# Counting a group once behind serial accumulating DMAs, and projecting in halves into the bank of the counts

## The chip, the core and the metric

The kernel runs on one core of one Trainium2 chip. The metric is the time of one execution on the device, in microseconds (us). Before the change the median of three runs is 3099.81 us (3097.14 to 3100.33). The core has five engines with a queue each, worked off in order: PE multiplies matrices into the output memory PSUM, which the kernel uses in banks of 512 float32 columns per partition; DVE and ACT work on its results and copy them out to SBUF; POOL adds tiles in SBUF and issues the accumulating DMAs; SP issues the other DMAs.

## The reference

Sixteen batches of 1024 rows and 256 columns go through two attention layers, each after a layer norm with ReLU, with a residual sum. Layer 0 has 4 heads, layer 1 has 8; the same 1024x1024 adjacency matrix of a batch masks both. Cut to what matters:

```python
h = max(layernorm(x), 0)
q, k, v = h @ Wq, h @ Wk, h @ Wv                  # per head
scores = where(adj > 0, q @ k.T / sqrt(D), -inf)
x = x + (softmax(scores) @ v) @ Wo + bo           # layer 0, then the same for layer 1
```

## The kernel before

All work is in float32, and the scores are kept transposed: keys lie on the partitions and 512 queries (one half `qh` of the rows) on the free axis. A **group** is one half of the queries and 128 of the 256 head columns (`g`): two heads of 64 columns in layer 0, four heads of 32 in layer 1. A layer of a batch thus has four groups, g0 to g3 in the order (qh 0, g 0), (0, 1), (1, 0), (1, 1). A group has 8 **steps** in layer 1 (4 in layer 0); a step makes four blocks of 128 keys by 512 queries.

What a step does: `scores` (L493 to L505) writes two pairs of banks from the pool `ps_s`, which has three pairs. `exponentials` masks each pair on DVE (L524) into a tile p, which frees the pair, and takes the exponential on ACT (L530). Two steps later (`LEAD`), `weigh` (L535) multiplies p by the values into the bank `po`. Even steps put their p into a tile of the pool tag `p0` with 7 buffers, odd ones into two half tiles of the tags `p10` and `p11` with 2 buffers each.

The softmax denominators are the sums of p over the keys. In layer 1 `count_steps` (L645) first has POOL add each odd step's p onto the even step's tile, in place (L659, two additions of 128x1024 each), after `weigh` has read both. That leaves four tiles per group, after the steps j = 1, 3, 5, 7. An accumulating DMA from POOL's queue (`accumulate`, L642) adds one such tile to another. `count` (L381) multiplies by a matrix of ones and so sums over the partitions; it writes the bank `pz`, which has a single buffer (the pool `ps_o` has one buffer per tag). `spread` (L404) copies that bank out on ACT (L407), sends the sums to another layout by DMA, and `invert` (L425), `fetch` and `normalize` (L447) take the reciprocal, bring it back and scale the group's output.

Before the change the groups g0, g1 and g2 of layer 1 are counted twice, once for j = 1 and 3 together and once for j = 5 and 7, and most of these counts are issued in two halves of 256 columns at successive steps (`halves`, L689). g3 is counted once. In layer 0 groups are added differently (`add_tiles`) and counted in pairs.

The inputs of a layer (norm, transpose, then `k`, `q` and `values` for each half of the rows) are made in steps of other batches. Norms are computed on ACT (L221) into one buffer `hn`, transposed in 32x32 blocks on DVE (L273), written to DRAM by a DMA as `turned` (L278) and read back as hT (L285). The projections `kq` (L289) and `values` (L341) each fill one pair of `ps_s`, with 4 matmul calls for k or q and 8 for values (a matmul call lies in the trace as two instructions), and ACT or DVE copies the pair out. `end_half` (L478) projects the finished half by Wo through a pair of `ps_s` too (py, L483).

The order of everything is written out by hand. Steps of all batches form one list: layer 0 of batch b+1 (16 steps), then layer 1 of batch b (32 steps), and so on. I call such a run of 32 layer-1 steps a **stage** and number its steps 0 to 31; step 32 is the first of the following layer 0. `later(i, f, ...)` files a function for step i, and `run` (L588) issues, for each step: the scores, the weighing of earlier steps, the due counts, the exponentials, the other due functions in the order in which they were filed, and last those named in `LARGE`. At an even step of layer 1 with a due function from `LARGE`, the weighing is put off to the next step. `gr.waits` and `at` give the distances from a group's last weighing to its counts and to spread, invert, fetch and normalize. The stage of batch b carries the layer-0 inputs of batch b+2, filed at c + ..., where c is the stage's step 0.

Of the kernel before, what the change touches and what calls it, by code (L numbers as in the profile page):

```python
# [21 lines left out]

LEAD = 2

LARGE = ("k", "q", "values", "end_half")
COUNTS = ("count", "count_added")


# [62 lines left out]
def fast_program(ctx, tc, a, w, loads, chk):  # L91
# [89 lines left out]
    class Inputs:  # L181
# [98 lines left out]
        def place_blocks(self, half):  # L280
# [3 lines left out]
            for k in range(4):  # L284
                nc.sync.dma_start(  # L285
                    hT[ts(k, 32)].rearrange("p c (g q) -> p c g q", q=P), blocks[k]
                )

        def kq(self, half, is_q):  # L289
            if half == 0 and not is_q:  # L290
                self.kT = actp.tile([P, 2, N], F32, tag="kT", name=f"kT_{self.n}")
                self.v = actp.tile([P, NT, E], F32, tag="v", name=f"v_{self.n}")
            if is_q:
                to = self.qT[half] = actp.tile(
                    [P, 2, 512], F32, tag="qT", bufs=3, name=f"qT_{self.n}_{half}"
                )
            else:
                to = self.kT[:, :, ts(half, 512)]
            wt = w.q if is_q else w.k
            pq = psum_pair(f"pq_{self.n}_{half}_{int(is_q)}")  # L300
            shared = self.layer == 0 and self.b == 0 and half == 0
            for m in range(2):
                for c in range(2):
                    nc.tensor.matmul(  # L304
                        pq[:, m, :], wt[self.layer][:, c, ts(m, P)], self.hT[half][:, c, :],
                        start=(c == 0), stop=(c == 1),
                    )
            if shared:
                nc.scalar.copy(to[:, 0, :], pq[:, 0, :])
                nc.vector.tensor_copy(to[:, 1, :], pq[:, 1, :])  # L310
            elif self.layer == 0:
                if is_q:
                    nc.vector.tensor_copy(to, pq)
                else:
                    nc.scalar.copy(to, pq)
            else:
                for m in range(2):
                    if is_q:
                        nc.vector.tensor_scalar_add(to[:, m, :], pq[:, m, :], w.bq[:, m : m + 1])
                    else:  # L320
                        nc.scalar.activation(
                            to[:, m, :], pq[:, m, :], AF.Identity, bias=w.bk[:, m : m + 1]
                        )

        def test(self):

            held = small.tile([P, 32], F32, tag="held", bufs=1, name=f"held_{self.n}")
            for i in range(self.sums.shape[1] // 32):
                for bound, op in ((SUM_MIN, ALU.is_ge), (SUM_MAX, ALU.is_le)):
# [2 lines left out]
                    )  # L332
                    nc.gpsimd.tensor_mul(chk, chk, held)

        def k(self, half):
            self.kq(half, False)

# [230 lines left out]
    class Stream:  # L568
# [76 lines left out]
        def count_steps(self, i, st):  # L645
# [7 lines left out]
            elif j % 2:  # L653
                one = self.steps[i - LEAD - 1].p
                if gr.last and not (gr.brief or gr.pairs) and j == 7:
                    self.accumulate(gr.two, gr.one)
                for k, of in enumerate(st.halves):
                    half = one[:, ts(k, 2), :]
                    nc.gpsimd.tensor_add(half, half, of)  # L659
                if gr.pairs and (st.last or gr.hurry):  # L660
                    self.later(i + 2, gr.count, one, j == 1, st.last)
                elif gr.pairs:
                    self.halves(i + 3, gr, one, j == 1, False)
                elif j == 1:
                    gr.one = one
                elif j == 3:
                    self.accumulate(one, gr.one)
                    gr.one = one
                    if not gr.last:
                        self.halves(i + gr.waits[0], gr, one, True, False)  # L670
                    if gr.brief:
                        self.later(i + 6, gr.count, one, True, False)
                elif gr.brief and j == 5:
                    self.halves(i + 5, gr, one, False, False)
                elif gr.brief:
                    self.later(i + 4, gr.count, one, False, st.last)
                elif j == 5:
                    gr.two = one
# [21 lines left out]
        def end_group(self, i, gr):  # L700
# [128 lines left out]
    def block_inputs(inp, half, turn, put, place, *at):  # L829

        later(turn, inp.turn_blocks, half)
        later(put, inp.put_blocks, half)
        later(place, inp.place_blocks, half)
        for i, f in zip(at, (inp.k, inp.q, inp.values)):
            later(i, f, half)


    for i, f, half in (0, inp.k, 1), (0, inp.values, 0), (0, inp.values, 1), (2, inp.q, 1):
# [16 lines left out]
    for b in range(B - 1):  # L855
# [5 lines left out]
            norms(mine, 1, a + 10, a + 11, a + 12, a + 13, whole=True)  # L861
            half_inputs(mine, 1, a + 15, c, c + 6, c + 2)
        else:
            norms(mine, 0, a - 20, a - 16, a - 15, a - 13, bias=a)
            block_inputs(mine, 0, a - 10, a - 8, a - 4, a, a + 2, a + 8)
            norms(mine, 1, a - 14, a - 10, a - 8, a - 6, bias=a + 6)
            block_inputs(mine, 1, a, a + 6, a + 7, c, c + (6 if b + 2 < B else 10), c + 2)
        for i, u in zip((0, 2, 4, 6, 7, 9, 11, 13), range(NT)):
            later(a + i, masks[b].second, u)
        if b + 2 < B:  # L870
# [2 lines left out]
            later(c, open_x, b + 2, 1)  # L873
            if b == 0:
                norms(other, 0, a + 12, a + 14, c, c + 1, bias=c + 34)
                block_inputs(other, 0, c + 2, c + 3, c + 4, c + 8, c + 16, c + 18)
                norms(other, 1, c + 3, c + 4, c + 6, c + 7, bias=c + 36)
                block_inputs(other, 1, c + 8, c + 9, c + 12, c + 22, c + 26, c + 30)
# [267 lines left out]
```

## Time and profile before

| | |
|---|---|
| median of the runs | 3099.81 us |
| profiled execution | 3096.61 us |
| its span, first to last instruction | 3094.8 us |
| granted TensorE clock | 0.999 of full |
| PE, DVE, ACT, POOL busy | 99%, 80%, 72%, 79% of the span |
| accumulating DMAs | 133, of 1 MB each |

The stages repeat: the same large item of a stage starts 189.4 us after that of the one before (438.37, 627.97 and 817.37 us for one py). Of these 189.4 us some 76 belong to the 16 steps of layer 0 and some 113 to the 32 steps of layer 1. In the timeline a row merges equal instructions that follow each other: start, time, engine, line, operation, tiles, shapes and number, and in brackets idle time before it with what ended it. The time of a step is read from the start of its scores to the start of the next step's scores. In the groups by shape, busy time counts overlapping instructions of one group once.

### The profile page before, as it was taken

Reading aid. Unit: us, or ns where it says so; the run is one execution under the profiler, and the core shown is the slowest. Engines: PE = TensorE matmul, PEld = TensorE weight load, DVE = VectorE, ACT = ScalarE, POOL = GpSimd, SP = SyncE. Lnnn points to the kernel's source line nnn. Section 1 sums busy time; section 2 is a strip of 40 time slices with the busy share of each in tenths; the row PEclk is TensorE's granted clock in tenths of the full one; section 3 lists DMA queues with packets and bytes.
Section 4 is the critical chain, followed back from the end, with each engine's and each line's share of the span. In section 5 each row is a group of like instructions: output and inputs, shape, how many; then the busy total and the mean of one; then the engine's idle time right before and its main releaser. Section 6 shows DMA issues by size and latency. Waiting matters only on the chain.

```text
span 3094.8 us, 47328 instructions
## 1 busy us (share of the span) xinstructions
PE 3074.0 (99%) x17406; PEld 1221.3 (39%) x17406; DVE 2474.6 (80%) x2698; ACT 2230.1 (72%) x2436; POOL 2436.5 (79%) x1554
## 2 busy tenths in 40 slices
PE   9999999999999999999999999999999999999998
PEld 4443433434334343343434334343343433434333
DVE  6778788887888878788787888878788787887777
ACT  5677777777777777778677677776777777776676
POOL 3578878787887878878788787887878778787787
PEclk9999999999999999999999999999999999999999
DMA  5215545454463544635445353554535545453331
GB/s 129 66 58 118 127 106 129 121 112 119 107 137 110 119 118 103 143 108 117 120 103 134 107 127 110 113 127 110 127 110 111 132 105 125 120 112 84 79 77 33
DMA packets 259230, 341.37 MB, mean 110 GB/s; under 512 B 58288, under 2 KB 218288, under 8 KB 241968
## 3 DMA queue, kind: packets, MB, share of 16 engines
q0 software_dynamic: 19152, 139.47, 22.6%
q1 hardware_dynamic: 238368, 197.51, 22.2%
q8 instruction: 138, 2.26, 0.3%
q10 hardware_dynamic: 1472, 1.31, 0.2%
q14 instruction: 100, 0.82, 0.1%
HBM read 149.95 MB, written 47.96 MB: 64 GB/s over the span
## 4 chain that ended last, share of the span: by engine, by line
PE 95%; DVE 2%; POOL 1%; DMA 1%; issue 1%; ACT 0%; SPq 0%; DVEq 0%; ACTq 0%; POOLq 0%
PE ps L501 31%; PE po L542 29%; PE pq L304 15%; PE pv L345 8%; PE py L483 7%; PE pz L387 4%; DVE p L524 1%; POOL p L659 1%; DMA inv<-vd 0%; DMA x<-in_x_dram 0%; SPq L420 0%; ACT p L530 0%; DMA sums<-s 0%; POOL cat L447 0%; DMA adj<-in_adj_dram 0%
## 5 line engine op out<-in xcount | busy, mean ns | idle before, releaser
L524 DVE SCALAR_TENSOR_TENSOR p<-mask,ps 128x1024 f32<-128x1024 fp8e5 x1536 | 1791.9, 1214 | 366.2 <-PE ps L501 348.5
L530 ACT ACTIVATE p<-p 128x1024 f32<-128x1024 f32 x1536 | 1607.0, 1056 | 628.1 <-DVE p L524 572.1
L659 POOL TENSOR_TENSOR p<-p,p 128x1024 f32<-128x1024 f32 x510 | 1212.8, 2430 | 166.3 <-PE po L542 165.8
L501 PE MATMUL ps<-qT,kT 32*128 32x512 f32 (+1 forms) x6144 | 1073.3, 628 | 3.6 <-DVE p L524 3.0
L542 PE MATMUL po<-p,v 128*32 128x512 f32 (+1 forms) x6144 | 980.2, 600 | 0.7 <-ACT cat L399 0.4
L501 PEld LDWEIGHTS ps<-qT,kT 32*128 32x128 f32 (+1 forms) x6144 | 349.7, 184 | 587.9 <-issue 243.1
L542 PEld LDWEIGHTS po<-p,v 128*32 128x32 f32 (+1 forms) x6144 | 234.3, 118 | 680.3 <-issue 474.5
L555 POOL TENSOR_TENSOR p<-p 128x1024 f32<-128x1024 f32 x128 | 302.7, 2365 | 90.5 <-DVE p L554 85.1
L554 POOL TENSOR_TENSOR p<-p,p 128x1024 f32<-128x1024 f32 x64 | 150.8, 2356 | 169.6 <-DVE p L551 126.3
L345 PE MATMUL pv<-wv,hT 128*128 128x256 f32 x1024 | 237.8, 385 | 0.0
L304 PE MATMUL pq<-hT,wk 128*128 128x512 f32 x512 | 236.7, 605 | 0.7 <-DVE p L524 0.6
L304 PE MATMUL pq<-hT,wq 128*128 128x512 f32 x512 | 236.6, 605 | 0.1
L483 PE MATMUL py<-wo,cat 128*128 128x256 f32 x1008 | 234.4, 386 | 0.7 <-DVE p L524 0.6
L447 POOL TENSOR_TENSOR cat<-cat,inv 128x512 f32<-128x512 f32 x127 | 174.9, 1383 | 73.0 <-DMA inv<-vd 72.6
L345 PEld LDWEIGHTS pv<-wv,hT 128*128 128x128 f32 x1024 | 189.4, 190 | 72.1 <-DVE p L524 21.3
L483 PEld LDWEIGHTS py<-wo,cat 128*128 128x128 f32 x1008 | 186.3, 190 | 74.8 <-issue 25.1
L551 DVE TENSOR_TENSOR p<-p 128x1024 f32<-128x1024 f32 x128 | 181.7, 1419 | 0.0
L387 PE MATMUL pz<-p,ones 128*32 128x256 f32 (+1 forms) x1928 | 180.4, 444 | 0.5 <-DMA p<-p 0.5
L643 POOL DMA_DIRECT2D p<-p x133 | 122.6, 922 | 63.7 <-POOL p L659 30.3
L221 ACT ACTIVATE hn<-x,shift,rstd 128x256 f32<-128x256 f32 x251 | 135.6, 588 | 43.7 <-DMA turned<-hn 32.2
L399 ACT COPY cat<-po 128x512 f32<-128x512 f32 x128 | 73.4, 573 | 118.5 <-PE py L483 96.6
L488 DVE TENSOR_TENSOR x<-py,x 128x1024 f32<-128x1024 f32 x63 | 77.1, 1224 | 101.9 <-PE py L483 101.2
(62 smaller groups left out, 1773.1 us busy)
## 6 DMA issues: line engine op xcount, KB each, us to landing
p<-p POOLq DMA_DIRECT2D x133, 1024.0 KB, 7.8
adj<-in_adj_dram SPq DMA_DIRECT2D x504, 128.0 KB, 3.0
turned<-hn SPq DMA_DIRECT2D x58, 512.0 KB, 3.8
hT<-turned SPq DMA_DIRECT2D x232, 128.0 KB, 2.8
x<-in_x_dram SPq DMA_DIRECT2D x128, 128.0 KB, 3.1
inv<-vd SPq DMA_DIRECT2D x128, 128.0 KB, 3.0
inv<-vd SPq DMA_DIRECT2D x252, 64.0 KB, 3.3
out_dram<-x SPq DMA_DIRECT2D x124, 128.0 KB, 2.3
```

What stands on the lines that cost most here:

```text
L304: nc.tensor.matmul(pq[:, m, :], wt[self.layer][:, c, ts(m, P)], self.hT[half][:, c, :], start=(c == 0), stop=(c == 1),)
L345: nc.tensor.matmul(pv[:, i, :], self.hT[half][:, c, ts(i, P)], w.v[self.layer][:, c, :], start=(c == 0), stop=(c == 1),)
L387: nc.tensor.matmul(self.s[ts(r, 32), q], w.ones.to_broadcast([P, 32]), of[:, q], start=start and not part, stop=stop and part != 0,)
L447: nc.gpsimd.tensor_mul(o, o, inv)
L483: nc.tensor.matmul(py[:, i, :], self.half.cat[:, c, ts(i, P)], w.o[self.layer][:, c, :], start=(c == 0), stop=(c == 1),)
L501: nc.tensor.matmul(st.ps[i // 2][:, i % 2, :], gr.inp.kT[r * D : (r + 1) * D, gr.g, ts(kt, P)], gr.inp.qT[gr.qh][r * D : (r + 1) * D, gr.g ...
L524: nc.vector.scalar_tensor_tensor(out=half, in0=gr.mask.m[gr.qh][:, kt // 4, :, kt % 4].unsqueeze(1).to_broadcast([P, 2, 512]), scalar=-EDG ...
L530: nc.scalar.activation(half, half, AF.Exp, scale=gr.scale)
L542: nc.tensor.matmul(gr.o[r * D : (r + 1) * D, :], gr.inp.v[:, kt, h * D : (h + 1) * D], st.halves[i // 2][:, i % 2, :], start=(kt == 0), st ...
L551: nc.vector.tensor_add(a, a, b)
L555: nc.gpsimd.tensor_add(a, a, b)
L659: nc.gpsimd.tensor_add(half, half, of)
```

## The change

For g0, g1 and g2 of layer 1 the four tiles are now added up completely before one count. At j = 3 and j = 5 the tile of the pair before is accumulated at once; at j = 7 the DMA is filed two steps later. g0 is counted whole 9 steps after its last weighing, g1 in two halves 9 and 10 steps after it, g2 whole 8 steps after it; g3 is as it was. Spread, invert and, for g1 and g2, fetch move accordingly.

In the layer-0 inputs of batches 2 to 15 four of the six projections are made in two parts each, at two steps: k of half 0 (steps 8 and 10), q of half 0 (14 and 16), k of half 1 (20 and 22) and values of half 1 (28 and 30). A part writes one bank, with the tag `pz` of the counts, instead of a pair of `ps_s`, and is copied out by itself. q of half 1 moves from step 26 to 24. Some statistics and norms of the layer-1 inputs move by one to three steps. The last batch's layer 1 (`pairs`) and the special case `brief` are as before.

```diff
-LARGE = ("k", "q", "values", "end_half")
+LARGE = ("k", "q", "values", "end_half", "k_part", "q_part", "values_part")
...
+        def part(self, half, is_q, m):
+
+            if m == 0 and is_q:
+                self.qT[half] = actp.tile(
+                    [P, 2, 512], F32, tag="qT", bufs=3, name=f"qT_{self.n}_{half}"
+                )
+            to = self.qT[half] if is_q else self.kT[:, :, ts(half, 512)]
+            wt = w.q if is_q else w.k
+            pq = ps_o.tile([P, 512], F32, tag="pz", name=f"pq_{self.n}_{half}_{int(is_q)}_{m}")
+            for c in range(2):
+                nc.tensor.matmul(
+                    pq, wt[self.layer][:, c, ts(m, P)], self.hT[half][:, c, :],
+                    start=(c == 0), stop=(c == 1),
+                )
+            (nc.vector.tensor_copy if is_q else nc.scalar.copy)(to[:, m, :], pq)
...
+        def values_part(self, half, m):
+            pv = ps_o.tile([P, 512], F32, tag="pz", name=f"pv_{self.n}_{half}_{m}")
+            pv = pv.rearrange("p (t e) -> p t e", e=E)
+            for i in range(2):
+                for c in range(2):
+                    nc.tensor.matmul(
+                        pv[:, i, :], self.hT[half][:, c, ts(2 * m + i, P)],
+                        w.v[self.layer][:, c, :], start=(c == 0), stop=(c == 1),
+                    )
+            nc.scalar.copy(self.v[:, 4 * half + 2 * m : 4 * half + 2 * m + 2, :], pv)
...
-            self.waits = ((5, 5), (7, 7), (7, 6), None)[2 * qh + g]
+            self.waits = (9, 9, 8, 4)[2 * qh + g]
...
-                elif not gr.last:
-                    self.accumulate(one, gr.two)
-                    if gr.qh:
-                        self.later(i + 6, gr.count, one, False, True)
+                elif not st.last:
+                    self.accumulate(one, gr.one)
+                    gr.one = one
+                else:
+                    of, k = (gr.two, 1) if gr.last else (gr.one, 2)
+                    self.later(i + k, self.accumulate, one, of)
+                    if gr.g and not gr.qh:
+                        self.halves(i + gr.waits, gr, one, True, True)
                     else:
-                        self.halves(i + gr.waits[1], gr, one, False, True)
-                else:
-                    self.later(i + 1, self.accumulate, one, gr.two)
-                    self.later(i + 4, gr.count, one, True, True)
+                        self.later(i + gr.waits, gr.count, one, True, True)
...
-                at = ((6, 12, 15, 19), (8, 12, 14, 17, 19), (6, 9, 11, 14), None)[2 * gr.qh + gr.g]
+                at = ((10, 13, 15, 19), (10, 14, 15, 18, 19), (8, 11, 12, 14), None)[2 * gr.qh + gr.g]
...
-            norms(mine, 0, a - 20, a - 16, a - 15, a - 13, bias=a)
+            norms(mine, 0, a - 22, a - 19, a - 15, a - 13, bias=a)
...
-            norms(mine, 1, a - 14, a - 10, a - 8, a - 6, bias=a + 6)
+            norms(mine, 1, a - 14, a - 13, a - 8, a - 6, bias=a + 6)
...
-                block_inputs(other, 0, c, c + 1, c + 2, c + 8, c + 16, c + 18)
+                block_inputs(other, 0, c, c + 1, c + 2, (c + 8, c + 10), (c + 14, c + 16), c + 18)
...
-                block_inputs(other, 1, c + 7, c + 8, c + 12, c + 22, c + 26, c + 30)
+                block_inputs(other, 1, c + 7, c + 8, c + 12, (c + 20, c + 22), c + 24, (c + 28, c + 30))
```

Here a = c + 32 is the first step of the layer 0 that follows the stage.

More of the change, by code (lines that the diff above doesn't have):

```diff
@@ L287, in place_blocks, with open_kv @@
                 )
+        def open_kv(self):
+            self.kT = actp.tile([P, 2, N], F32, tag="kT", name=f"kT_{self.n}")
+            self.v = actp.tile([P, NT, E], F32, tag="v", name=f"v_{self.n}")
         def kq(self, half, is_q):
             if half == 0 and not is_q:
-                self.kT = actp.tile([P, 2, N], F32, tag="kT", name=f"kT_{self.n}")
-                self.v = actp.tile([P, NT, E], F32, tag="v", name=f"v_{self.n}")
+                self.open_kv()
             if is_q:
@@ L333, in test, with k_part, q_part @@
                     nc.gpsimd.tensor_mul(chk, chk, held)
+        def part(self, half, is_q, m):
[12 more added lines that the diff above has]
+            (nc.vector.tensor_copy if is_q else nc.scalar.copy)(to[:, m, :], pq)
+        def k_part(self, half, m):
+            if half == 0 and m == 0:
+                self.open_kv()
+            self.part(half, False, m)
+        def q_part(self, half, m):
+            self.part(half, True, m)
+        def values_part(self, half, m):
[8 more added lines that the diff above has]
+            nc.scalar.copy(self.v[:, 4 * half + 2 * m : 4 * half + 2 * m + 2, :], pv)
         def k(self, half):
@@ L665, in count_steps @@
                     gr.one = one
-                elif j == 3:
+                elif gr.brief:
+                    if j == 3:
+                        self.accumulate(one, gr.one)
+                        self.later(i + 6, gr.count, one, True, False)
+                    elif j == 5:
+                        self.halves(i + 5, gr, one, False, False)
+                    else:
+                        self.later(i + 4, gr.count, one, False, True)
+                elif gr.last and j == 5:
+                    gr.two = one
+                elif not st.last:
                     self.accumulate(one, gr.one)
                     gr.one = one
[L669 to L678, printed above, removed]
-                elif not gr.last:
-                    self.accumulate(one, gr.two)
-                    if gr.qh:
-                        self.later(i + 6, gr.count, one, False, True)
-                    else:
-                        self.halves(i + gr.waits[1], gr, one, False, True)
-                else:
-                    self.later(i + 1, self.accumulate, one, gr.two)
-                    self.later(i + 4, gr.count, one, True, True)
+                else:
+                    of, k = (gr.two, 1) if gr.last else (gr.one, 2)
+                    self.later(i + k, self.accumulate, one, of)
+                    if gr.g and not gr.qh:
+                        self.halves(i + gr.waits, gr, one, True, True)
+                    else:
+                        self.later(i + gr.waits, gr.count, one, True, True)
         def halves(self, i, gr, one, start, stop):
@@ L833, in block_inputs @@
         later(place, inp.place_blocks, half)
-        for i, f in zip(at, (inp.k, inp.q, inp.values)):
-            later(i, f, half)
+        parts = inp.k_part, inp.q_part, inp.values_part
+        for i, f, part in zip(at, (inp.k, inp.q, inp.values), parts):
+            if type(i) is tuple:
+                for m in range(2):
+                    later(i[m], part, half, m)
+            else:
+                later(i, f, half)
     for i, f, half in (0, inp.k, 1), (0, inp.values, 0), (0, inp.values, 1), (2, inp.q, 1):
@@ L875, in fast_program @@
                 norms(other, 0, a + 12, a + 14, c, c + 1, bias=c + 34)
[L876 removed]
+                block_inputs(other, 0, c + 2, c + 3, c + 4, (c + 8, c + 10), (c + 14, c + 16), c + 18)
                 norms(other, 1, c + 3, c + 4, c + 6, c + 7, bias=c + 36)
[L878 removed]
+                block_inputs(other, 1, c + 8, c + 9, c + 12, (c + 20, c + 22), c + 24, (c + 28, c + 30))
             else:
                 norms(other, 0, a + 10, a + 12, a + 13, a + 15, bias=c + 34)
[L881 removed]
+                block_inputs(other, 0, c, c + 1, c + 2, (c + 8, c + 10), (c + 14, c + 16), c + 18)
                 norms(other, 1, c + 2, c + 4, c + 5, c + 6, bias=c + 36)
[L883 removed]
+                block_inputs(other, 1, c + 7, c + 8, c + 12, (c + 20, c + 22), c + 24, (c + 28, c + 30))
             at = 5, 8, 10, 12, 14, 45, 49, 51, 53
```

## The prediction

> **What bounds the kernel now.** I read the page's busy shares first, then the chain of work that ended last, then the groups kept apart by shape, then the timelines of one stage, engine by engine.
>
> ```profile
> PE 3074.0 (99%) x17406; PEld 1221.3 (39%) x17406; DVE 2474.6 (80%) x2698; ACT 2230.1 (72%) x2436; POOL 2436.5 (79%) x1554
> PE ps L501 31%; PE po L542 29%; PE pq L304 15%; PE pv L345 8%; PE py L483 7%; PE pz L387 4%; DVE p L524 1%; POOL p L659 1%; DMA inv<-vd 0%; DMA x<-in_x_dram 0%; SPq L420 0%; ACT p L530 0%; DMA sums<-s 0%; POOL cat L447 0%; DMA adj<-in_adj_dram 0%
> p<-p POOLq DMA_DIRECT2D x133, 1024.0 KB, 7.8
> ```
>
> PE is busy 99% of the span and is 95% of the chain: PE work taken out is time won, and every wait put into PE's queue is time lost. The accumulating DMA (last line) lands 7.8 us after issue.
>
> ```profile
> L387 PE MATMUL pz<-p,ones 128*32 128x256 f32 x1360 | 106.1, 379 | 0.5 <-DMA p<-p 0.5
> L387 PE MATMUL pz<-p,ones 128*32 128x512 f32 x568 | 75.1, 600 | 0.0
> ```
>
> These are the counts, in halves and whole. Their busy time overlaps their neighbours', so I price them from PE's timeline, in a layer-1 stage whose step 0 is at 959.63, step 8 at 992.90, step 12 at 1005.61:
>
> ```profile
> 1005.61 1.15 PE L501 MATMUL ps<-qT,kT 32*128 32x512 f32 x8
> 1006.77 3.72 PE L483 MATMUL py<-wo,cat 128*128 128x256 f32 x16
> 1010.42 1.14 PE L501 MATMUL ps<-qT,kT 32*128 32x512 f32 x8
> 1011.49 1.92 PE L542 MATMUL po<-p,v 128*32 128x512 f32 x16
> 1013.34 1.14 PE L501 MATMUL ps<-qT,kT 32*128 32x512 f32 x8
> 1014.41 1.07 PE L542 MATMUL po<-p,v 128*32 128x512 f32 x8
> 1015.29 0.61 PE L387 MATMUL pz<-p,ones 128*32 128x256 f32 x8
> 1015.84 1.14 PE L501 MATMUL ps<-qT,kT 32*128 32x512 f32 x8
> 1017.79 0.61 PE L387 MATMUL pz<-p,ones 128*32 128x256 f32 x8
> 1018.34 1.15 PE L501 MATMUL ps<-qT,kT 32*128 32x512 f32 x8
> ```
>
> From start to start: a step with a large item (scores, then py, pq or pv) takes 4.7 to 4.8 us (L); the next, with the weighing of two steps, 2.92 (W); a step with one weighing and half a count 2.50 (H). No step is shorter than DVE's two masked minima (2.35 together). ACT and POOL in the same stage:
>
> ```profile
> 1018.34 2.19 ACT L530 ACTIVATE p<-p 128x1024 f32<-128x1024 f32 x2 [0.38 <-DVE p L524]
> 1020.43 0.57 ACT L407 COPY s<-pz 128x512 f32<-128x512 f32 x1
> 1054.78 1.09 ACT L221 ACTIVATE hn<-x,shift,rstd 128x256 f32<-128x256 f32 x2 [3.77 <-DMA turned<-hn]
> ```
>
> ```profile
> 989.64 0.93 POOL L643 DMA_DIRECT2D p<-p  x1 [0.30 <-POOL p L659]
> 992.27 4.70 POOL L659 TENSOR_TENSOR p<-p,p 128x1024 f32<-128x1024 f32 x2 [1.70 <-PE po L542]
> 996.94 2.50 POOL L447 TENSOR_TENSOR cat<-cat,inv 128x512 f32<-128x512 f32 x2
> 999.89 4.72 POOL L659 TENSOR_TENSOR p<-p,p 128x1024 f32<-128x1024 f32 x2 [0.45 <-PE po L542]
> ```
>
> ```profile
> p<-p POOLq DMA_DIRECT2D x2, 1024.0 KB, 9.4
> turned<-hn SPq DMA_DIRECT2D x1, 512.0 KB, 11.3
> ```
>
> The reader should see three things: the copy of the counts stands behind its step's exponentials and ends 2.7 us into the next step (1021.0 against 1018.34); POOL has only 0.45 us of idle time before the additions at 999.89; and when an accumulating DMA meets the transposed-tile DMA (1042.7 and 1043.4), both land after 11 to 12 us, and ACT sits 3.77 us.
>
> **The change, part by part, for one stage.**
>
> *Counts removed.* A stage gives up 8 half counts and gains one whole one. A half adds 0.46 (0.88+0.55 with it, 0.97 without); a whole one 0.88 (the 1.74+0.97 around 1072.50, against 1.85). 8 x 0.46 - 0.88 = 2.8 us less PE work.
>
> *Projections in halves.* A part is 4 matmul instructions, half of the 3.65, so a part step takes 1.07+1.83 = 2.90 (A). Because part steps count as large, the weighing goes to the next step. PE's queue from step 8 to 32 becomes 8 A, 11 W, 2 H and the L at 12, 18, 24: 23.2+32.1+5.0+14.2, and whole counts at 18 and, moved over the stage's end, 33: 1.8. Sum 76.3, against 79.8 (steps 8 to 32 repeat every 189.4 us; 80.6 in this one). **Won: 3.5 us per stage, if nothing waits.** The copies in halves cost ACT 3 x (2x0.57-1.0) and DVE 2x0.69-1.22, under 0.6 together, beside PE's work: nothing. If that cover went, ACT's 0.4 would stand in the next item.
>
> *The bank of the counts, group 0.* The bank has one buffer. The group's count is in step 18, the copy that frees it in step 19, the part of k in step 20, with nothing between. In ACT's queue the copy is behind step 19's two exponentials and two norms (L221). From the start of 19, by the distances at step 9 to 10 of this stage (scores 997.61 and 1000.53, minima 998.85, exponentials 1002.96 for 2.19): DVE starts at 1.2, exponentials 2.45 to 4.64, norms to 5.7, copy to 6.25. PE wants the bank at 2.92+1.07 = 4.0. **Added: 2.3 us**; without the norms 1.2, with a late ACT 2.7. All later PE work stands behind the waiting matmul.
>
> *The same for group 1.* Second half of the count and copy in step 27, part of values in 28. From the start of 27: step 26's exponentials end at 2.15, norms 3.2, exponentials 5.3, copy 5.85; PE wants it at 2.49+1.07: 2.2 us (1.6 at the least). But step 24's norms overwrite the tile that the DMA `turned` reads. Now that DMA lands 16 us after step 22 began (1038.69, 1054.68). In the change two steps after 22 take 5.8, not 7.7, and g2's first accumulating DMA again starts beside it. So ACT resumes 10.2 after step 24, reaches the copy 9 us later (2 norms, 6 exponentials, a copy of po, 2 norms, the copy), at 19.2; PE wants it at 14.3: 4.9 us. An undisturbed transfer (5 us) gives 2.2. **I take 4.0**, nearer to the collision, which the trace shows.
>
> *Accumulation.* Per stage 3 more DMAs: 0.9 each of POOL (0.3 before, 0.6 to the next). The one at j=5 must wait for the one at j=3 to land, and POOL's additions stand behind it. At step 7: issue 989.64, landing 997.5, next POOL work 998.6; normalize (2.50) to 1001.1; the additions end at 1005.8 rather than 1004.6, while PE is 1.5 us earlier at step 11. They free the p buffer for step 11's second minimum: done 1007.05; py in step 12 wants that score buffer at 1005.7. Wait 1.5; 0.4 without POOL's part, since the stats moved to step 10 delay DVE too; 0 if DVE catches up. **I take 1.0.** At step 24 (0 to 0.6, transpose in step 22) **0.3**. Later POOL lateness is covered by the waits above; without them it would cost 0 to 3. SP's queue has the same 682 entries; its sums go one step later with the copies, and normalize has 5 steps of cover.
>
> The Trainium skill ("DMA: Bandwidth & Descriptors", Anatomy of one DMA) fits a GpSimd-issued DMA as 2.0 us plus bytes over 436 GB/s, by which 1 MB lands after an estimated 4.4 us and POOL would not wait at all. The trace has 7.8; by the page the sum would be about 0.6 us per stage smaller.
>
> The skill's "PSUM — Partial Sum Buffer" (Summary: rules for kernel authors) says to evacuate promptly and to read a bank other than the one matmuls write; it speaks against sharing this bank. It gives no time.
>
> *Sum.* -3.5 + 2.3 + 4.0 + 1.0 + 0.3 = +4.1 us per stage. Parts exist in 14 stages (layer-0 inputs of batches 2 to 15): +57. Batch 14's stage has new counts without parts; its short steps become DVE-bound: -1. +56 on the profiled execution's 3096.6 gives 3153, and the median of the runs lies 3.2 above that execution: **3156 us**.
>
> **Rivals.** *Faster: the bank is free in time.* If ACT runs the copies ahead of PE's need, and the buffers absorb POOL's waits, 3.5 x 15 = 52 us go: 3047. For it: PE idles hardly at all now. Against: 1021.0. It decides once all waits of a stage are below 3.5. *Half of it: the two bank waits at their least* (1.2+1.6) and nothing else: -0.7 per stage, 3089. *POOL's chain decides:* the counts' DMA waits grow to 11 us and each group loses 3 more: 4.1+3 per stage, 3198. For it: POOL is busy 68.5 of 79.8. *No change:* waits equal gain, 3100.
>
> **Numbers.** Slower as worked out 0.66, POOL deciding 0.12, no change 0.06, the least waits 0.08, all free 0.08. From these: slower 0.78, within 0.2% (6 us, about what runs of this kernel can tell) 0.06, faster 0.16. The bounds of the waits (0+1.2+1.6+0 = 2.8 to 1.5+2.7+4.9+0.6 = 9.7 per stage, less 3.5) give 3089 to 3186; I take 3085 to 3195, which leaves out the free case and half of POOL's.
>
> **What would show it.** PE waits for the copy of the counts (ACT s) ahead of k parts in step 20 and values parts in 28, some 2 and 4 us, 14 times each; PE's busy share falls to about 96%; 178 accumulating DMAs, and POOL waiting on them about 40 times. Whole counts 688, halves 400. It is wrong if PE stays at 99%, or if its waits are on DVE alone.

## The result, and the profile after

The changed kernel takes 3211.48 us (median of four runs, 3207.59 to 3217.17), the kernel before beside it 3099.72: a ratio of 1.0368, 95% interval 1.0355 to 1.038. It is 112 us slower; 56 were forecast. The page of its profiled execution (span 3209.3 us) has these two lines for those shown of before:

```profile
PE 3081.2 (96%) x16566; PEld 1212.4 (38%) x16566; DVE 2485.0 (77%) x2712; ACT 2243.5 (70%) x2478; POOL 2477.0 (77%) x1599
...
p<-p POOLq DMA_DIRECT2D x178, 1024.0 KB, 8.1
```

PE is busy for 7 us more than before, with 840 fewer matmul instructions: a busy share alone doesn't show that work went. The view of PE's waits (engine, line, releaser: total us, times, longest) shows most of the idle time, 122 us against 14.7 before:

```profile
PE pq L348 <- ACT s L445: 29.8, 14, 2.1
PE pv L367 <- ACT s L445: 23.1, 14, 2.8
PE ps L539 <- DVE p L562: 22.2, 24, 1.5
PE py L521 <- DVE p L562: 17.8, 15, 1.2
PE po L580 <- ACT cat L437: 13.7, 14, 1.1
```

The first two are the waits for the bank of the counts, the fourth is py in step 12; the third and the fifth were not forecast. To see all of the time, I added up PE's timeline by product, each from the start of a run of matmuls to the start of the next run, so that waits and stretched rows are in and the sum is the span without its head:

| us | before | after | only the counts changed (`e5_counts_only`) |
|---|---|---|---|
| counts (pz) | 164.4 | 113.9 | 112.9 |
| scores, layer 1 | 568.7 | 675.7 | 649.3 |
| scores, layer 0 | 471.8 | 492.0 | 498.3 |
| k and q (pq) | 464.1 | 474.0 | 465.7 |
| py | 238.1 | 254.8 | 246.5 |
| weighing, layer 1 | 466.7 | 473.5 | 482.5 |
| values (pv) | 233.2 | 235.9 | 233.2 |

The counts gave back 50 us, as promised, and everything that follows them took 165. (A wait stands in the row of the product before it: the wait of a k part in the scores.) By place: the time up to the first layer-1 stage grew by 1.4 us, the 14 stages with parts and the layer-0 runs between them by 102.7, what follows by 10.4. Mean step times over the 14 stages, and over the 13 layer-0 runs between them (start of scores to start of the next scores):

| step | before | after | what ended the new wait |
|---|---|---|---|
| part steps 8, 10, 14, 16, 22, 30 | | 2.98 to 3.00 | none |
| 12 | 4.80 | 8.00 | DVE, behind POOL, behind a DMA |
| 20 | 2.50 | 5.30 | ACT, copy of the counts |
| 24 and 25 | 2.50, 2.50 | 4.80, 2.92 | none; q moved here |
| 26 | 4.78 | 3.52 | ACT, copy of po |
| 28 | 2.54 | 4.75 | ACT, copy of the counts |
| 8 to 32 | 79.94 | 84.91 | |
| layer 0 that follows | 76.53 | 78.95 | DVE, behind a DMA of the sums (1.5); the rest is g2's count, moved there |

**Step 12.** The timeline of one stage, whose step 12 starts at 1033.77 (start, time, engine, operation, in brackets the idle time before and its releaser):

```profile
1018.51 0.94 POOL L681 DMA_DIRECT2D p<-p  x1 [0.30 <-POOL p L697]
1027.59 0.89 POOL L681 DMA_DIRECT2D p<-p  x1 [1.74 <-DMA p<-p]
1028.20 2.82 POOL L485 TENSOR_TENSOR cat<-cat,inv 128x512 f32<-128x512 f32 x2
1030.67 9.62 POOL L697 TENSOR_TENSOR p<-p,p 128x1024 f32<-128x1024 f32 x4
1033.38 1.22 DVE L562 SCALAR_TENSOR_TENSOR p<-mask,ps 128x1024 f32<-128x1024 fp8e5 x1 [0.76 <-POOL p L697]
1033.77 2.01 PE L539 MATMUL ps<-qT,kT 32*128 32x512 f32 x8
1035.69 3.48 DVE L562 SCALAR_TENSOR_TENSOR p<-mask,ps 128x1024 f32<-128x1024 fp8e5 x3 [1.09 <-POOL p L697]
1036.97 5.41 PE L521 MATMUL py<-wo,cat 128*128 128x256 f32 x16 [1.19 <-DVE p L562]
```

This is the chain of the prediction, link by link: POOL's DMA of j = 5 stands until that of j = 3 (1018.51) has landed, normalize and the additions are late, DVE's minima wait for the tile that an addition frees, the scores lie 2.01 instead of 1.14 and py waits 1.19. New is the length of py, 5.41 against 3.72. Two stages in the view by window (PE, PEld, DVE, ACT and POOL busy, then the granted clock, DMA share, GB/s), step 12 each time:

```profile
836.38:843.18 6.80, 5.62 (x28) 3.56 (x24) 4.27 (x4) 4.23 (x4) 6.80 (x4) 1.00 0.48 95
1033.77:1042.30 8.53, 7.34 (x28) 4.69 (x24) 4.31 (x4) 4.23 (x4) 7.34 (x4) 0.80 0.50 95
```

The waits are the same; in the second the clock was granted at 0.80 on average (0.50 from 1037.29 to 1040.70; half of these 3.41 us is the 1.7 by which py is longer). In 9 of the 14 stages step 12 has a clock of 0.80 to 0.82 and takes 8.4 to 9.4 us, in 5 it has 1.00 and takes 6.2 to 6.8. The chain itself thus costs 1.8, the clock 1.4 on the mean.

**Steps 20, 26 and 28.**

```profile
1067.44 1.08 ACT L221 ACTIVATE hn<-x,shift,rstd 128x256 f32<-128x256 f32 x2
1068.42 0.56 ACT L445 COPY s<-pz 128x512 f32<-128x512 f32 x1
1069.04 1.98 PE L348 MATMUL pq<-hT,wk 128*128 128x512 f32 x4 [2.12 <-ACT s L445]
...
1087.19 1.09 ACT L221 ACTIVATE hn<-x,shift,rstd 128x256 f32<-128x256 f32 x2 [2.79 <-DMA turned<-hn]
1088.19 1.04 ACT L568 ACTIVATE p<-p 128x1024 f32<-128x1024 f32 x1
1089.14 0.56 ACT L437 COPY cat<-po 128x512 f32<-128x512 f32 x1
1089.75 1.06 PE L580 MATMUL po<-p,v 128*32 128x512 f32 x8 [1.10 <-ACT cat L437]
...
1095.77 0.57 ACT L445 COPY s<-pz 128x512 f32<-128x512 f32 x1
1096.39 1.99 PE L367 MATMUL pv<-wv,hT 128*128 128x256 f32 x8 [1.56 <-ACT s L445]
```

The first three lines are step 20 as forecast, the last two step 28. At 1087.19 the norms wait for the DMA that reads their tile, as forecast; but behind them in ACT's queue stands the copy of po too, and with q moved to step 24 the weighing of the next group in step 26 wants that bank at once. That wait comes first and uses up part of what step 28 would have waited.

**Layer 0.** SP's queue and what hangs on it, after:

```profile
1141.80 2.49 SPq L152 DMA_DIRECT2D adj<-in_adj_dram  x4
1144.33 1.98 SPq L477 DMA_DIRECT2D inv<-vd  x4
1146.41 2.44 SPq L458 DMA_DIRECT2D sums<-s  x4
1150.19 0.25 DVE L466 RECIPROCAL vn<-sums 128x16 f32<-128x16 f32 x1 [2.79 <-DMA sums<-s]
1151.58 1.13 PE L539 MATMUL ps<-qT,kT 64*128 64x512 f32 x4 [1.54 <-DVE p L562]
```

and the same place before:

```profile
1095.83 2.20 SPq L439 DMA_DIRECT2D inv<-vd  x4
1107.19 2.49 SPq L152 DMA_DIRECT2D adj<-in_adj_dram  x4
1109.78 2.44 SPq L420 DMA_DIRECT2D sums<-s  x4
1113.59 0.25 DVE L428 RECIPROCAL vn<-sums 128x16 f32<-128x16 f32 x1 [0.82 <-DMA sums<-s]
```

g2's fetch (inv) stood ahead of the adjacency loads and now stands behind them, so g3's sums leave 2 us later; the reciprocal that waits for them blocks the minima in DVE's queue, and PE waits 1.54 for a score buffer, once in each of the 13 layer-0 runs between the stages.

### The profile page after: what moved, and what is told of

Same layout as the page of the kernel before. It is cut to its first block, busy times and chain, and to the rows that moved or that the text cites. A ratio compares the mean times of both kernels' runs of the same rounds, so it can differ in the third digit from the quotient of the medians.

```text
span 3209.3 us, 45826 instructions
## 1 busy us (share of the span) xinstructions
PE 3081.2 (96%) x16566; PEld 1212.4 (38%) x16566; DVE 2485.0 (77%) x2712; ACT 2243.5 (70%) x2478; POOL 2477.0 (77%) x1599
## 5 line engine op out<-in xcount | busy, mean ns | idle before, releaser
L697 POOL TENSOR_TENSOR p<-p,p 128x1024 f32<-128x1024 f32 x510 | 1216.4, 2479 | 168.5 <-PE po L580 166.8
L539 PE MATMUL ps<-qT,kT 32*128 32x512 f32 (+1 forms) x6144 | 1097.3, 628 | 22.9 <-DVE p L562 22.2
L580 PE MATMUL po<-p,v 128*32 128x512 f32 (+1 forms) x6144 | 967.1, 599 | 13.7 <-ACT cat L437 13.7
L681 POOL DMA_DIRECT2D p<-p x178 | 170.4, 957 | 152.2 <-DMA p<-p 114.5
L521 PE MATMUL py<-wo,cat 128*128 128x256 f32 x1008 | 249.6, 403 | 19.9 <-DVE p L562 17.8
L592 POOL TENSOR_TENSOR p<-p,p 128x1024 f32<-128x1024 f32 x64 | 150.7, 2355 | 147.1 <-DVE p L589 124.6
L589 DVE TENSOR_TENSOR p<-p 128x1024 f32<-128x1024 f32 x128 | 199.1, 1555 | 0.0
L383 PE MATMUL pv<-wv,hT 128*128 128x256 f32 x800 | 185.7, 385 | 1.1 <-DVE p L562 1.1
L307 PE MATMUL pq<-hT,wq 128*128 128x512 f32 x400 | 184.8, 605 | 0.8 <-DVE p L562 0.8
L383 PEld LDWEIGHTS pv<-wv,hT 128*128 128x128 f32 x800 | 148.0, 190 | 58.3 <-issue 24.4
L230 POOL TENSOR_TENSOR x<-x,bo 128x1024 f32<-128x1024 f32 x64 | 156.1, 2512 | 0.0
L595 POOL TENSOR_TENSOR p<-p,p 128x1024 f32<-128x1024 f32 x64 | 151.7, 2370 | 5.0
```

Of the source, the lines that this page charges most:

```text
L307: nc.tensor.matmul(pq[:, m, :], wt[self.layer][:, c, ts(m, P)], self.hT[half][:, c, :], start=(c == 0), stop=(c == 1),)
L383: nc.tensor.matmul(pv[:, i, :], self.hT[half][:, c, ts(i, P)], w.v[self.layer][:, c, :], start=(c == 0), stop=(c == 1),)
L521: nc.tensor.matmul(py[:, i, :], self.half.cat[:, c, ts(i, P)], w.o[self.layer][:, c, :], start=(c == 0), stop=(c == 1),)
L539: nc.tensor.matmul(st.ps[i // 2][:, i % 2, :], gr.inp.kT[r * D : (r + 1) * D, gr.g, ts(kt, P)], gr.inp.qT[gr.qh][r * D : (r + 1) * D, gr.g ...
L580: nc.tensor.matmul(gr.o[r * D : (r + 1) * D, :], gr.inp.v[:, kt, h * D : (h + 1) * D], st.halves[i // 2][:, i % 2, :], start=(kt == 0), st ...
L589: nc.vector.tensor_add(a, a, b)
```

## The experiments

Unless another is named, an edit is made to the changed kernel; "stage" is steps 8 to 32, means over 14; layer 0 is the mean over 13.

**One wait at a time.** The copy of g0's counts one step earlier:

```diff
-at = ((10, 13, 15, 19), ...
+at = ((9, 13, 15, 19), ...
```

> The changed kernel, with the copy of g0's counts out of its bank (spread) filed one step earlier, in step 18 with the count itself; invert, fetch and normalize stay. In the changed kernel step 20 takes 5.18 us, 2.2 more than the other steps with a part (2.98). Bank theory: the wait in step 20 is the wait for this copy, so step 20 falls to about 3.0 and the time by 14 x 2.2 = 31 us, to about 3180. POOL theory (POOL's lateness sets the stage, and a wait taken out in one place comes back in another): step 20 falls but later steps or step 12 grow, and the time stays within 8 us of 3211.

3216.64 us, 1.0385 [1.0365, 1.0404]. Step 20 falls from 5.30 to 2.98, so its wait was this copy and nothing else; but step 28 rises from 4.75 to 7.77, the stage stays at 84.92. The time was not won but moved: step 20's wait had kept PE behind ACT. In 13 of the 14 stages the clock in step 28 is 0.74 to 0.90.

Accumulating in pairs, so that no DMA waits for the one before it:

```diff
-elif gr.last and j == 5:
+elif j == 5:                      # gr.two = one, no DMA
...
-    of, k = (gr.two, 1) if gr.last else (gr.one, 2)
-    self.later(i + k, self.accumulate, one, of)
+    self.accumulate(one, gr.two)                        # j == 7
+    self.later(i + 3, self.accumulate, one, gr.one)     # g3 as it was
```

> The changed kernel, with the accumulating DMAs of g0 to g2 as a tree: j=3 takes j=1 at once, j=7 takes j=5 at once, and only the last one, j=3 into j=7, waits for others and is filed three steps later. As many DMAs (178), as few counts; the DMA at j=5 that waits for the landing of the one at j=3 in POOL's queue is gone. POOL theory: the additions of step 9 end 1.5 to 2.5 us earlier, step 12 falls from 8.5 to between 4.8 and 5.5 (its wait and the 1.7 us at half clock that follow from it), and the time falls by 42 to 52 us to 3160 to 3170. Bank theory alone: step 12 stays above 7 and the time above 3195.

3194.1 us, 1.0315 [1.0298, 1.0332]. Step 12 falls from 8.00 to 4.81, with a clock of 1.00 in every stage: the serial DMA, and the half clock behind it, were all of its 3.2 us. The time falls by 17 us only, not by the 42 to 52 expected: steps 18, 20 and 21 together rise by 0.7, and layer 0 by 0.9, where PE now waits for ACT's copy of kT.

g2's fetch ahead of the adjacency loads again:

```diff
-(8, 11, 12, 14)
+(8, 10, 11, 14)
```

> The changed kernel, with g2's invert and fetch one step earlier (10 and 11 steps after its last weighing instead of 11 and 12), so that SP's queue has these four DMAs ahead of the adjacency loads again, as before the change. Queue theory: the sums of g3 then go out 2 us earlier, DVE's reciprocal no longer waits for them 2.8 us ahead of a score minimum, PE's wait of 1.54 us in the layer 0 after each stage goes, and the time falls by 14 x 1.5 = 21 us to about 3190. If that wait comes from POOL or ACT being late instead, the time stays within 6 us of 3211.

3182.56 us, 1.0272 [1.0255, 1.0289]: 29 us for one place in SP's queue. Layer 0 falls from 78.95 to 77.21, and PE's waits for DVE ahead of scores from 22.2 to 3.6 us in the whole run.

The parts in half a pair of score buffers:

```diff
-pq = ps_o.tile([P, 512], F32, tag="pz", ...)
+pq = psum_pair(...)[:, 0, :]      # pv alike
```

> The changed kernel, with each part written to half of a pair of score banks instead of the bank of the counts; steps, halves and copies stay. Bank theory: the waits in steps 20 (2.2 us) and 28 (1.65) go, 14 x 3.85 = 54 us, and 3157 is left if the score pairs can spare a part. Rival (the score pairs are as scarce as the bank): each of 8 parts delays the next scores by about 0.5 us, 14 x 4 = 56 us, and the time stays near 3211.

3204.0 us, 1.0344 [1.0327, 1.0361]. Both bank waits go (step 20: 3.08, step 28: 3.32), but steps 9, 15, 21 grow to some 4.0 and 11, 17, 23, 31 to 3.5: the scores now find no free pair. Although both waits and most of step 12's excess (5.35) go, the stage takes only 0.6 less.

The norms behind which po's copy stands, two steps later:

```diff
-norms(mine, 1, a - 14, a - 13, a - 8, a - 6, ...)
+norms(mine, 1, a - 14, a - 13, a - 6, a - 4, ...)
```

> The changed kernel with one edit: the norms of the second half of the layer-1 inputs in steps 26 and 28 instead of 24 and 26. Theory: in step 24 they wait for the DMA of the tile they overwrite and hold up, behind them on ACT, the copy of g2's output that frees the bank po; PE's wait of 1.0 us in step 26 for that copy goes (step 26 from 3.5 to 2.6). The copy of g1's counts stands behind as many ACT instructions as before from step 26 on, so step 28 stays at 4.6 or more: the time falls by about 13 us to 3198, or not at all if the wait comes back in step 28 as it did when only g0's copy was moved.

3207.99 us, 1.0342 [1.0325, 1.036]. Step 26 falls from 3.52 to 2.59, so the copy of po was behind these norms; step 28 rises from 4.75 to 5.40. Again the wait went on to the next place.

**The counts without the halves.** Projections whole and at the steps of before, statistics and norms as before; the new counts and their DMAs stay.

```diff
-(c + 8, c + 10), (c + 14, c + 16), c + 18
+c + 8, c + 16, c + 18
-(c + 20, c + 22), c + 24, (c + 28, c + 30)
+c + 22, c + 26, c + 30
```

> The new counting and accumulation alone: all six projections whole, in pairs of score banks, at the steps of the kernel before, and its steps for statistics and norms. Theory: POOL's wait for the DMA at j=5 has room here, because step 8 keeps its whole projection (4.7 us); what is left of the loss is the wait behind SP's queue in layer 0 (1.5 x 14 = 21 us). The ten steps that gave up half a count or more cannot get much below DVE's 2.35 us, so of the 2.8 us of PE work only about 1 is won and whole counts in steps 18 and 33 give it back: 3115 to 3135. Rival (the serial DMAs by themselves make the loss): 3160 or more, with step 12 above 6 us.

3175.09 us, 1.0243 [1.0226, 1.026], above the 3115 to 3135 that I expected and where the rival had it. Two thirds of the loss come with the counting alone, its DMAs and its places in the queues: step 12 takes 7.26, POOL waits 44 times for a landing (128.3 us), and the last column of the table above shows that PE's 51 us come back in the scores of layer 1, and 29 more.

**All of it together.** Pairwise accumulation, both earlier places, and g1's count one step earlier with its norms at steps 27 and 29; then the same without the pairs:

```diff
-self.waits = (9, 9, 8, 4)
+self.waits = (9, 8, 8, 4)
-at = ((10, 13, 15, 19), (10, 14, 15, 18, 19), (8, 11, 12, 14), None)
+at = ((9, 13, 15, 19), (9, 14, 15, 18, 19), (8, 10, 11, 14), None)
-norms(mine, 1, a - 14, a - 13, a - 8, a - 6, ...)
+norms(mine, 1, a - 14, a - 13, a - 5, a - 3, ...)
```

> The changed kernel with four edits together: the accumulating DMAs as a tree, g2's invert and fetch one step earlier, the copy of g0's counts in step 18, and for g1 the half counts in steps 25 and 26, the copy in step 26 and the norms of step 24 and 26 in 27 and 29. If each wait is what it was said to be, no step waits: steps 8 to 32 take about 77 us (79.9 before the change, 84.9 changed), layer 0 and the count in it 77.3 (76.5 before), and the time is about 3097 - 14 x 2.1 = 3068. If a wait that is taken out only moves (as from step 20 to 28), steps 8 to 32 stay above 80 us and the time above 3100.

3136.85 us, 1.0127 [1.011, 1.0144]. The stage takes 77.89, 2.05 less than before the change, of which 0.9 is g2's count, which moved to layer 0: some 1.2 is what halves and counts are worth in it with nearly all waits gone. But layer 0 takes 80.50, 4.0 more than before, 3.1 without that count.

> The same four-edit kernel without the tree: the serial DMAs of the changed kernel stay. POOL theory: step 12 is back at 6 to 8 us, POOL is late again at the later groups, and the time is 14 x 2 to 3.5 us = 28 to 50 us above the kernel with the tree. If the serial DMAs cost nothing once the bank is free, both agree within 8 us.

3143.83 us, 1.0145 [1.0128, 1.0162]: 7 us above the kernel with the pairs, not 28 to 50. Step 12 is back at 7.47 and the stage at 80.66, as the theory has it, but layer 0 is at 78.23. So 2.3 us of layer 0 come with the pairs. In the run with all edits g3's first DMA leaves in the flight of g2's third, and the timeline at the start of layer 0 reads:

```profile
1274.51 0.87 POOL L681 DMA_DIRECT2D p<-p  x1 [0.30 <-POOL p L697]
1285.75 0.87 POOL L681 DMA_DIRECT2D p<-p  x1 [5.61 <-PE ps L539]
1286.36 4.98 POOL L697 TENSOR_TENSOR p<-p,p 128x1024 f32<-128x1024 f32 x2
1289.05 1.22 DVE L562 SCALAR_TENSOR_TENSOR p<-mask,ps 128x1024 f32<-128x1024 fp8e5 x1 [1.35 <-POOL p L697]
1299.22 2.26 PE L539 MATMUL ps<-qT,kT 64*128 64x512 f32 x8 [1.37 <-DVE qT L322]
```

The second DMA of g3 must follow the first, and PE is named as its releaser though PE was done; POOL sits 5.6 us, DVE is late behind its additions, PE behind DVE.

**Pairs for g0 and g1 alone.** The edits of `e6_all` with g2 serial again, and the same with whole projections and the norms of before:

```diff
-elif j == 5:
+elif j == 5 and (gr.last or not gr.qh):      # g2 serial again
```

> All edits of the run with everything mended, but the pairwise accumulation only for g0 and g1; g2 keeps its serial DMAs. Theory: the 80.5 us of layer 0 in that run come from g2's third DMA, issued a step later and into the flight of g3's first one (5.9 us apart, the second landed after 11.2 us), so POOL's additions free p late and DVE is late for layer 0. Then layer 0 falls back to some 78.2, step 12 stays at 4.9, steps 8 to 32 take some 78.1 to 78.5: 2.0 us per stage less, about 3108 us (3100 to 3118). Rival: layer 0 is late because the layer-1 stage got 3 us shorter and POOL, whose work did not shrink, is simply behind: then layer 0 stays at 80 or more and the time near 3135.

3120.73 us, 1.0072 [1.0059, 1.0086], 3 above the range given. Layer 0 is at 78.23, step 12 at 4.98, as the theory has it; the stage at 78.98 misses by 0.5, for step 28 is now at 4.01, by the chain of step 12 once more, in g2:

```profile
1245.62 0.87 POOL L681 DMA_DIRECT2D p<-p  x1 [0.30 <-POOL p L697]
1254.76 0.87 POOL L681 DMA_DIRECT2D p<-p  x1 [3.56 <-DMA p<-p]
1255.36 9.64 POOL L697 TENSOR_TENSOR p<-p,p 128x1024 f32<-128x1024 f32 x4
1258.07 1.22 DVE L562 SCALAR_TENSOR_TENSOR p<-mask,ps 128x1024 f32<-128x1024 fp8e5 x1 [0.75 <-POOL p L697]
```

> The same counts, DMAs and positions with the six projections whole and at their steps of before: what the halves are worth once the counts' DMAs are in order. Theory: with whole projections alone steps 8 to 32 took 82.1, of which step 12 gives back 2.4, and layer 0 some 78: 3110 to 3125 us, so 5 to 15 us slower than the run with halves. Rival: the halves bring nothing and cost PE time in their part steps (2.98 + 2.92 against 4.75 + 2.92 + 2.07 for whole ones, and one whole projection less often held by DVE's 2.35): then this run is equal or faster, below 3108.

3132.75 us, 1.0118 [1.0103, 1.0134]: 12 us slower than with halves (the theory's 5 to 15), though the run lies 8 above the range given. That the halves themselves are worth these 12 us is not shown, for step 16 takes 6.30 (4.97 in `e5_counts_only`), 14 x 1.3 = 19 us, by the chain of step 12 in g1:

```profile
1215.16 0.87 POOL L681 DMA_DIRECT2D p<-p  x1 [2.73 <-DMA p<-p]
1220.79 3.48 DVE L562 SCALAR_TENSOR_TENSOR p<-mask,ps 128x1024 f32<-128x1024 fp8e5 x3 [1.09 <-POOL p L697]
1222.07 3.70 PE L307 MATMUL pq<-hT,wq 128*128 128x512 f32 x8 [1.19 <-DVE p L562]
```

With halves the same lateness costs 0.4, in step 18. Without them the counts save 50 us of PE's time and the scores of layer 1 take 59 more. DVE in that run, steps 24 to 26:

```profile
1250.84 7.29 DVE L562 SCALAR_TENSOR_TENSOR p<-mask,ps 128x1024 f32<-128x1024 fp8e5 x6 [0.50 <-PE ps L539]
```

Six minima without a gap. A step without its half count takes PE 2.07 us, and DVE needs 2.35 for its two minima, so the next steps are longer: steps 20 to 22 take 9.48 us together against 9.81 before, 0.33 less where two half counts of 0.46 are gone. Most of what a half count costs is work that PE did while DVE had to be waited for anyway.

**POOL's load.** Layer 1's normalize left out (its output is not divided by its sums), in the run with pairs for g0 and g1 and in the kernel before:

```diff
 def normalize(self):
+    if self.layer:
+        return
```

> The run with pairwise accumulation for g0 and g1, with layer 1's normalize left out (the output of layer 1 is not divided by its sums): POOL loses 4 multiplications of 1.28 us a stage and its waits for the fetched reciprocals (77 us in all in the run with everything mended); PE, DVE and ACT keep all their work. Theory: DVE's 92.6 us of waiting for POOL's additions is what keeps that version above the kernel before; with POOL 5 to 10 us a stage lighter those waits mostly go, steps 24, 25, 28 and 29 fall by 1 to 2 us together and layer 0 by 0.6: 3080 to 3102 us against 3121. Rival: DVE's own time, or the copies on ACT, hold those steps: then it stays within 8 us of 3121.

> The kernel before with the same cut, the control: there DVE waits 4.5 us in all for POOL's additions and PE idles 14.7 us. Theory: 3085 to 3100 us, no more than 0.4% below the uncut kernel, so that the gain of the other run is one of the change and not of the cut. Rival: the kernel before gains as much as the changed one, 15 us or more; then POOL's load says nothing about the change.

3100.31 us, 1.0006 [0.9997, 1.0016], and 3097.43, 0.9998 [0.9988, 1.0007]. The sizes are those of the theory, the places are not: steps 24, 25, 28 and 29 are as they were (4.92, 3.36, 4.00, 3.38), layer 0 fell from 78.23 to 77.29 and the end by 8 us. So a lighter POOL helps the changed kernel and not the one before, but not in step 28, where POOL sits out a landing, as the fence above shows.

**Spacing, and the end.** The edits of `e7_all_but_tree`, all DMAs serial, that of j = 5 one step later; then the same with batch 14, whose stage has no parts, counted as before:

```diff
+if j == 5:
+    self.later(i + 1, self.accumulate, one, gr.one)
+else:
     self.accumulate(one, gr.one)
```

> All edits of the run with everything mended but the pairwise accumulation; in its place the DMAs stay serial and the one at j = 5 is issued one step later, three steps behind that at j = 3. Theory (spacing): POOL waits for landings no more than 25 times instead of 42, step 12 falls to 4.8 to 5.2 and step 28 to 3.0 to 3.5, steps 8 to 32 take 77 to 78, layer 0 stays at 78.2: 3090 to 3110 us. Rival (POOL has too little time for a third DMA per group): the wait moves to the DMA at j = 7 or to the buffers of p, and steps 12 or 28 stay above 6 or 4: 3120 us or more, as without the delay.

> The same with batch 14, whose stage has no halves, counted as before. In the changed kernel the time behind the 14 stages with halves is 323.5 us against 313.1. Theory: those 10 us are the price of counts taken out of steps that are then shorter than DVE's two minima, so this run is 8 to 14 us faster than the one with which it runs. Rival: they come from the end of the last stage with halves (a late POOL, layer 0): then less than 4 us.

3112.13 us, 1.0049 [1.0035, 1.0062], and 3105.32, 1.0022 [1.0013, 1.0032]. One step of distance brings step 12 from 7.47 to 5.32 without any pairs; step 28 stays at 3.71 and POOL still waits 27 times, so the theory's 3090 to 3110 is missed by 2. Batch 14 is worth 7 us, a little under the 8 to 14 expected (the time behind the 14 stages falls from 324.6 to 316.5). So the counts alone cost time there, but not in the place that the theory named: batch 14's own stage takes 112.96 us with the new counts and 112.74 with the old ones, short steps and all. The gain is in the first five steps of the last batch behind it (29.2 to 22.1 us), where with the new counts POOL's additions, DVE's minima and a normalize are late (PE waits 2.4 for that normalize).

**The last two costs.** In that last run g0 alone in pairs, and then also the copy of g2's counts one step later, behind the copies of kT in layer 0, for which PE waits 0.59:

```diff
-(8, 10, 11, 14)
+(9, 10, 11, 14)
```

> The run with spaced DMAs and batch 14 as before, with g0 alone accumulated pairwise. Theory: step 12 falls from 5.37 to 4.9, step 18 stays at 5.72 (it rose only where g1 was pairwise too): 0.4 us per stage, 3098 to 3102 us. Rival: as with the pairwise g0 and g1 together, step 18 takes it back: 3105 us.

> The same, with the copy of g2's counts one step later, behind the copies of kT. Theory: the second item of layer 0 falls from 11.70 by the 0.59 us that PE waits for kT, to some 11.1: 8 us less than its neighbour, 3090 to 3094 us, which would be faster than the kernel before. Rival: the sums then come too late for the reciprocal one step on, DVE waits for them, and layer 0 is no shorter than 78.2: the time stays at its neighbour's or rises.

3106.6 us, 1.0027 [1.0017, 1.0036]: step 12 4.91, but step 18 6.13, the rival; no gain. And 3222.01 us, 1.0393 [1.0379, 1.0407]: the wait for kT did go (the item fell from 11.71 to 11.22), but the reciprocal comes one step on and now waits for the sums, with the copy of qT behind it:

```profile
1333.07 2.50 SPq L459 DMA_DIRECT2D sums<-s  x4
...
1342.39 0.25 DVE L467 RECIPROCAL vn<-sums 128x16 f32<-128x16 f32 x1 [7.12 <-DMA sums<-s]
...
1343.93 3.78 PE L540 MATMUL ps<-qT,kT 64*128 64x512 f32 x8 [6.20 <-DVE qT L322]
```

PE waits 88.2 us for that copy in the whole run: one step in one queue cost 115 us. The trace shows with what these sums, four DMAs of 2 KB, land: one step later they are issued around one of POOL's accumulating DMAs (at 1333.49). The first two, issued at 1333.07 and 1333.67, land after 1.7 us; the last two, 0.8 and 1.4 us behind it, after 6.2 and 7.2, the last 0.2 us after the large one has landed (1341.97). It is so in all 14 stages (6.1 to 7.4 us).

No version that divides by its sums is faster than the kernel before. The nearest is 0.22% above it.

## Why the direction came out and the size did not

The direction was right, and for the reason given: waits worth more than the PE work removed. Per stage with the layer 0 that follows, 4.1 us were forecast and 7.5 came (5.1 in layer 1, 2.4 in layer 0). In the forecast's terms: -2.8 + 2.3 + 2.8 + 3.2 + 1.5 = 7.0, and 0.5 in small rises of other steps, where it had -3.5 + 2.3 + 4.0 + 1.3. By the steps of the sum:

- **Counts removed**: right. 688 whole and 400 half counts; 50 us off PE, where -2.8 in each of 15 stages makes 42.
- **Projections in halves**: a part step takes 2.98, not 2.90, eight times a stage, and the large steps 4.80 and 5.72: the work is 0.9 more than forecast. Eight parts, 11 steps of 2.92, the large ones at 4.80, 5.72 and 4.80 and two of 2.50 make 76.3 for steps 8 to 32 without waits, against 79.94 before; with the count in step 33 that is 2.8 won, not 3.5, so this mis-sizing alone leaves a gain.
- **Group 0's bank, 2.3**: right, 2.1 of wait and 2.3 in the step.
- **Group 1's bank, 4.0**: mis-sized and in part misplaced. ACT did sit out the DMA `turned`, but 2.7 to 2.8 rather than the collision's 3.8 us: the stage read for the prediction was one of the two worst of 14 (the others had 2.0 to 2.9), and in the changed kernel the DMA landed after 8.0 us, not 11.3. The first to feel it was the weighing in step 26, for po's copy stands behind the same norms: 1.0 there, 1.8 in step 28 over their unhindered times, 2.8 in all.
- **Accumulation, 1.0 at step 12 (0 to 1.5)**: the step that failed most. The chain was right in every link; it cost 3.2. The wait and the stretched scores are 1.8, a little past the bound of 1.5 (for which its own times, 1007.05 and 1005.7, give 1.35), and the half clock behind them adds 1.4, which no row of the trace before shows. The 0.3 at step 24 did not come (4.80, no wait).
- **"SP's queue has the same 682 entries; its sums go one step later with the copies, and normalize has 5 steps of cover"**: failed, 1.5 us per stage taken as nothing. The number of entries was the wrong thing to count (by the traces SP issues 1922 DMAs in both kernels). Their order changed (fetch behind the adjacency loads), and the one with no cover was not normalize but the reciprocal on DVE, ahead of minima.
- **Batch 14's stage, -1**: wrong in sign. What follows the 14 stages lost 10.4: 0.9 in a layer 0, 3.6 in batch 14's stage and 6.0 in the steps of the last batch behind it. With spaced DMAs batch 14's new counts cost some 7 (`e14_spaced_old_tail`), all of it behind the stage. The forecast looked at the stage alone and left out that POOL would be late behind it; what the 3.6 in the stage are was not separated.

Of the rivals, POOL's chain (3198) came nearest in number, not in mechanism: the landing is 8.1 in the median, not 11, and only in step 12, for one group of a stage, did it reach PE at once. The estimate by the Trainium skill's "DMA: Bandwidth & Descriptors" (Anatomy of one DMA; 4.4 us to landing, POOL never waiting) is contradicted: POOL waited 41 times, 114.5 us. The advice of its "PSUM — Partial Sum Buffer" (Summary: rules for kernel authors) to evacuate promptly, and to read another bank than the one that matmuls write, fits both bank waits. But with the parts in other banks only 7 us of the 112 came back, since the score buffers were then short. The signs promised came true (two bank waits 14 times each, though the second is 1.6 us and not 4, PE at 96%, 178 DMAs, 41 waits); they did not tell 56 from 112.

## What to carry to other kernels

In a kernel whose engines are all 70 to 99% busy, work removed from the bounding engine is worth only what the next engine leaves of it: compare each shortened step with that engine's time for the same step before the saving is booked. A moved step changes the order in every queue that it issues to; for each of its entries ask what it now stands behind, and what stands behind the instruction that waits for it. And if removing a wait makes another appear one place on, the lateness belongs to a slower chain: lengthen the distance in that chain (one step for a DMA that lands after 8 us) instead of mending the places where it shows.

## What was not expected of the hardware

The granted clock of PE fell to 0.50 for 3.41 us within step 12, behind a wait of only 1.19 us and scores stretched by 0.7 to 1.8 us, in 9 of 14 stages; behind the longer wait of step 20 (2.12 us, in all 14) it fell in one. So the length of the idle time does not decide alone, and equal stages differ by 2 us. The Trainium skill ("TensorE: Matmul & The Clock Gate", Why this matters for your kernels) advises no idle gaps above some 3 us between bursts of matmuls; here less was enough, with quarter-height scores (32 of 128 rows) before the gap. When the wait went (`e2_tree`), the clock was 1.00 in that step of all 14 stages.

The trace suggests that it is a matter of phase. The spells at 0.50 in the stages all last 3.41 us and start whole multiples of 3.413 us apart (870.04, 1037.29 and 1235.26: 49 and 58 of them). On that grid the 3.41 us ahead of a spell begin, in all nine stages, between 0.36 us before and 0.53 us after the start of step 12, so that the stretched scores and the wait lie almost whole in one such stretch. In four of the other five stages the grid cuts them apart (its nearest point is 0.48 us before the step, or 1.0 to 1.2 off), and in the fifth the scores were stretched by 0.2 only. In step 20 the clock fell in the one stage where a stretch begins with the step (0.03 us before it; 0.6 or more off in the others). No run shifts the phase on purpose, so what exactly trips it is not shown.

A small DMA can land late behind a large one: sums of 2 KB that land after 1.7 us took 6.1 to 7.4 when issued 0.8 to 1.7 us behind an accumulating DMA of 1 MB (`e16_and_spread_later`, 28 of 28).
